# A two-layer graph network on one core: a diagonal put behind two sums, a product order, and two steps moved by one

## The chip, the cores and the metric

The kernel runs on one core of a Trainium2 chip. The metric is the device time of one execution in microseconds (us); the times shown are medians of runs. The engines of the core are TensorE (PE in the profile, its weight loads PEld), VectorE (DVE), ScalarE (ACT), GpSimd (POOL) and SyncE (SP, whose queue issues nearly all DMAs). [...]

## The reference

Sixteen graphs of 1024 nodes with 512 features share one weighted adjacency matrix. Everything is float32.

```python
# x (16, 1024, 512), adj (1024, 1024), symmetric pattern with a diagonal
h = relu(layernorm(x))                         # without scale and shift
x = x + (adj @ h) @ weight + bias              # layer 0

h  = relu(layernorm(x))                        # layer 1
g  = h @ W
s1 = g @ a[:512]; s2 = g @ a[512:]
e  = leaky_relu(s1[:, :, None] + s2[:, None, :], 0.2) * adj
x  = x + elu(softmax(e, axis=2) @ g + beta * g)
```

## The kernel before, in words

All big products are done by a scheme with seven block products in place of eight (p1 to p7, in the order p1, p2, p6, p5, p7, p3, p4 in `PRODUCTS`): a matrix is cut into 2 x 2 blocks, sums of blocks (S1 to S4 of the left side, T1 to T4 of the right) are multiplied, and the results C11, C12, C21, C22 are sums of the products. Some products use the scheme once more inside (`inner_steps`, seven small products r1 to r7).

**Layer 0** goes over the 16 batches. For each, `layer0_a2` (`layer0_a` for the first) forms adjacency times h, by pairs of products whose inner steps alternate (`products_a2`), and `layer0_b` multiplies the result by the weight (`Weighted.rest`). Tiles of this stage are called `y_...` (`y_p1y` is the PSUM tile of p1's inner products, `y_p1t` what is kept of it) and `po_...`.

**Layer 1** then goes over the 16 batches again, in `layer1`. It uses softmax(e) @ h @ W. The exponentials stay unnormalised and transposed in blocks B11, B12, B21, B22 (`pT`). `beta` times a row's sum is added onto the diagonal of these blocks (`Softmax.diagonal`), so that one product gives both terms, and rows are divided by their sums (`rs`) in the last step. `products_a` multiplies this by the normalised features (`ul_U`, `ul_S`), in tiles `z_...`; the weighted products `pq_...` follow.

The last of these, p4, is made by the seven inner steps. `with_weighted` (line 259) runs them, and one or two matmul steps of the first weighted product after each:

```python
for m in range(7):
    inn[m]()
    reads(m)
    if m > 4:
        read.last(6 - m)
    next(steps)()
    ...
    after(m)
```

For p4 the inner order is r1, r2, r5, r4, r6, r3, r7. At m = 5 (r3) VectorE forms the second block of C21 (`z_C<-z_Y,z_p4t`) and `read.last(1)` takes S4's second block from it (`z_S<-z_C,z_S`). At m = 6 (r7) ScalarE copies r7's PSUM tile, VectorE adds to it (`z_p4t<-z_p4t,in`), forms C21's first block and S4's.

The weighted products go on in `Weighted.rest`: eight matmul calls each, four for each half q of the rows, in an order of their own. It is `P5_EARLY` (p1, p5, p2, p6, p7, p3, p4) for batches 0 to 14 and `NODES_LAST` for batch 15. p5 multiplies S1 into new PSUM banks of the kind X, p2 multiplies C21 into the banks W, which p1's result has been copied to. When a half is done, `done` (line 977) acts: for p6 and p5 ScalarE copies the bank (`part`); for p7 and p3 VectorE adds the bank to such a copy (`rest`); and `elu` follows for the four output quarters.

**Order of the work around it.** While batch b is multiplied, the softmax of batch b + 1 is made on ScalarE and VectorE. Which of its steps is issued where is written out by hand: dictionaries give for a step number k a list of names, and `after(k)` issues them, after the matmuls and reads of that step. In `SOFTMAX_A` and `SOFTMAX_B` (lines 1202 to 1207) M is masking and maximum, E an exponential of 128 rows, V its transposition, X and x the exchange of maxima by DMA, N and n their use, S and s the exchange of sums, D and d the diagonals of the first and second half, T1a to T4b the right sums. Step numbers of `plan_a` count 2 for a product, so the inner steps m = 0 to 6 of p4 are 12 to 18; those of `plan_b` begin at 2 with the first product after p1. D is these instructions on VectorE (lines 857 to 869): a reduction of the exchanged sums (`sall`), a reciprocal, a product with beta, and four additions onto diagonal blocks.

Line 1309 moves the entries 0 and 1 of `plan_b` to steps 17 and 18 of `plan_a`: before the change these are D at 17 and T1a at 18.

The softmax of layer 1's first batch is prepared during layer 0 (`EARLY_B`), kept in DRAM, and finished in layer 0's last batch by `FIRST_A` and `FIRST_B`, whose steps stand among the inner steps of `products_a2` (seven for each pair of products, counted from 0). R0 to R7 reload a kept tile by a DMA on SP's queue (`er<-ed`), E and V are as above; `exp` is four activations on ScalarE, V two transpositions on VectorE.

Instructions of VectorE, ScalarE, TensorE, GpSimd and SP are kept in the program's order (class `InOrder`), and all are recorded under its line, 119. So rows of the profile are told apart by the tiles, not by lines.

Of the kernel before, what the change touches and what calls it, by code (L numbers as in the profile page):

```python
# [55 lines left out]

FORKED = tuple((*p[:4], p[4] and p[0] != "p2", p[5]) for p in PRODUCTS)

NODES_LAST = tuple(FORKED[k] for k in (0, 1, 2, 3, 5, 4, 6))

P5_EARLY = tuple(FORKED[k] for k in (0, 3, 1, 2, 4, 5, 6))

# [4 lines left out]
def kernel(  # L67
# [12 lines left out]
    B, N, D = x.shape  # L80
# [255 lines left out]
    class Weighted:  # L336
# [17 lines left out]
        def steps(self, n, left):  # L354

            prod, _, bn, kind, first, last = self.products[n]
            first = first and (kind, 0) not in self.banks

            def step(q, i, dc):
                if first and i == 0 and dc == 0:  # L360
                    self.banks[kind, q] = bank(f"{self.name}_{kind}{q}")
                ps = self.banks[kind, q].rearrange("p (i o) -> p i o", i=2)
                pe.matmul(
                    ps[:, i, :], left[:, dc, ts(2 * q + i, P)], self.w[:, W_BLOCK[bn], dc, :],
                    start=(first and i == 0 and dc == 0), stop=(last and dc == 1),
                    skip_group_check=True,
                )
                if i and dc:
                    self.done(prod, q, ps)

            return [partial(step, q, i, dc) for q in range(2) for i in range(2) for dc in range(2)]
# [538 lines left out]
    def layer1(b, plan_a, plan):  # L910
# [52 lines left out]

        products = NODES_LAST if end else P5_EARLY
        at = {p[0]: 2 * n for n, p in enumerate(products)}
# [153 lines left out]
    def merged(*plans):  # L1119
        out = {}  # L1120
        for plan in plans:
            for k, steps in plan.items():
                out.setdefault(k, []).extend(steps)
        return out
# [26 lines left out]
    def plan_out(o, b):  # L1151

        return steps(
            (-1, o.keep, 0, 1), (-1, o.keep, 1, 0), (-1, o.keep, 1, 1), (0, o.relu, 0, 0),
            (1, o.stats, 1, 0, 0), (3, o.relu, 0, 1), (4, o.stats, 1, 0, 1), (7, o.relu, 1, 0),
            (8, o.stats, 1, 1, 0), (10, o.stats, 1, 1, 1), (13, o.relu, 1, 1),
            (2, o.logits, 0, 0, 0), (3, o.logits, 0, 0, 1), (7, o.logits, 0, 1, 0),
            (8, o.logits, 0, 1, 1), (9, o.logits, 1, 0, 0), (10, inner_left, b, "p7"),
            (12, o.logits, 1, 0, 1), (13, inner_left, b, "p3"), (15, o.logits, 1, 1, 0),
            (16, o.logits, 1, 1, 1), (16, o.store_logits), (18, inner_left, b, "p4"),  # L1160
            (3, o.store, 0, 0), (6, o.store, 0, 1), (10, o.store, 1, 0), (15, o.store, 1, 1),
            (18, begin, b, "Y"), (24, begin, b, "X"),
            (8, load_res, b, 0, 0), (10, load_res, b, 0, 1), (14, load_res, b, 1, 0),
            (18, load_res, b, 1, 1),
        )
# [16 lines left out]
    def plan_softmax(order, s):  # L1182
        names = {
            "L": [s.logits], "B": [s.blocks, 0], "b": [s.blocks, 1],
            "X": [s.spread_max, 0], "x": [s.spread_max, 1], "N": [s.top, 0], "n": [s.top, 1],
            "S": [s.spread_sum, 0], "s": [s.spread_sum, 1],
            "D": [s.diagonal, 0], "d": [s.diagonal, 1],
        }
        for g in range(NCH):
            names[f"M{g}"] = [s.masked, g]  # L1190
            names[f"E{g}"] = [s.exp, g]
            names[f"V{g}"] = [s.turn, g]
            names[f"L{g}"] = [s.load, g]
            names[f"e{g}"] = [s.load, g, b4, "b4"]
            names[f"K{g}"] = [s.keep, g]
            names[f"R{g}"] = [s.reload, g]
        for n in ("T1", "T2", "T3", "T4"):
            for k in range(2):
                names[n + "ab"[k]] = [s.right_sum, n, k]
        return {k: [tuple(names[n]) for n in steps.split()] for k, steps in order.items()}  # L1200
# [3 lines left out]
        6: "N B E0", 7: "E1 V0", 8: "E2 V1", 9: "n b E3 V2 S", 10: "E4 V3", 11: "E5 E6 V4",  # L1204
        12: "E7 V5", 13: "V6 s", 15: "V7",
    }
    SOFTMAX_B = {0: "D", 1: "T1a", 2: "T1b", 4: "d", 5: "T2a", 6: "T2b"}
    LOGITS_B = {8: "L", 9: "L0", 10: "L1", 11: "e2", 12: "e3"}
    LATE_A = {5: "T3a T4a", 6: "T3b T4b"}

# [7 lines left out]
        13: {9: "N n"},  # L1218
    }
    FIRST_A = {  # L1220
        -1: "R0", 4: "E0", 8: "B V0 R1", 10: "E1", 12: "V1 R2", 17: "E2", 18: "V2 R3", 23: "E3",
        25: "b", 26: "V3 R4 R5",
    }
    FIRST_B = {
# [8 lines left out]
    for b in range(B):  # L1233
        plans = [plan_out(out_of, b)] if b else []
# [23 lines left out]
        if b == 0:  # L1258
            plan_b = merged(
                {  # L1260
                    0: [(logit_weights_back, 0), (logit_weights_back, 1)],
                    1: [(inner_right, "p7", 1)], 2: [(inner_right, "p3", 1)],
                    3: [(inner_right, "p4", 1)],
                },
                *plans_b,
            )
            layer0_a(b, merged(plan_first(), at_end(merged(*plans))))
        else:
            plan_b = merged(*plans_b)
# [10 lines left out]
    for b in range(B):  # L1280
        plans = [{
            k - 14: [(f,) for f in later.pop(k)] for k in sorted(later)
        }]
        plans.append(plan_softmax(LATE_A, sms[b]))
        plans.append(steps((7, p4_right, b, 0), (8, p4_right, b, 1), (8, p4_left, b)))
        plans.append(steps((3, u_sums, b, 0, 1), (4, u_sums, b, 1, 1)))
        plan_b = {}
        if b == 0:
            plans += [
                {6: [(w_sums, w1_c)]}, steps((-1, u_sums, b, 0, 0), (0, u_sums, b, 1, 0)),  # L1290
            ]
        if b + 1 < B:
            plans.append(plan_softmax(SOFTMAX_A, sms[b + 1]))
            plans.append({k: [(load_u, b + 1, n)] for k, n in LOADS_U.items()})
            plan_b = plan_softmax(SOFTMAX_B, sms[b + 1])
        else:
            plans.append({7 + i: [(load_x1, b, nh, q)] for i, (nh, q) in enumerate(halves)})
        if b + 2 < B:
            plan_b = merged(plan_b, plan_softmax(LOGITS_B, sms[b + 2]))
        if 1 <= b <= NCH:  # L1300
            plan_b = merged(plan_b, {
                4: [(late.load, b - 1)], 9: [(late.stats,)], 10: [(late.relu,)],
                11: [(late.logits, b - 1)], 13: [(late.store,)],
            })
            if b == NCH:
                plan_b[13].append((late.store_logits,))
        if b + 1 < B:
            plan_b = merged(plan_b, steps((10, u_sums, b + 1, 0, 0), (12, u_sums, b + 1, 1, 0)))
        plans.append({k: plan_b.pop(i) for k, i in ((17, 0), (18, 1)) if i in plan_b})
        layer1(b, merged(*plans), plan_b)  # L1310
    for k in sorted(later):
        for f in later[k]:
# [34 lines left out]
```

## Time and profile before

| | |
|---|---|
| median of 3 runs | 2280.45 us (2279.64 to 2281.96) |
| profiled execution | 2280.27 us |
| its span | 2278.4 us |
| TensorE clock granted | 0.999 |
| TensorE, busy | 2240.0 us (98%) |
| weight loads, busy | 1647.0 us (72%) |
| VectorE, busy | 1950.5 us (86%) |
| ScalarE, busy | 1547.7 us (68%) |
| GpSimd, busy | 242.9 us (11%) |
| DMA, moved | 336.07 MB |

A row of the profile names engine, operation, the tile written and the tiles read, their sizes, and how often. In lists of waits the columns are: who waited, for whom, us in total, times, the longest. In a timeline they are start and duration in us, engine, line, operation, tiles, sizes, count, and in brackets the idle time of the engine ahead of it and who ended it. Matmuls are pipelined and their ends are modelled. The span runs from the first to the last instruction; the execution's own time has 1.87 us more around it.

### The profile page before, as it was taken

The numbers are of one execution on the slowest core, as the hardware profiler recorded it, in microseconds if no ns is written. First come the engines' busy times: TensorE is split into PE (matmuls) and PEld (weight loads), VectorE is DVE, ScalarE is ACT, GpSimd is POOL, SyncE is SP. The second block draws the span as 40 slices with busy tenths as digits, with TensorE's granted clock in tenths as the row PEclk, the third lists the DMA queues.
The fourth block names the chain that finished last, engine by engine and source line by source line (L and its number), as shares of the span: only waits on it lengthen the run. The fifth ranks groups of instructions, "written<-read, shape, count | busy, mean of one in ns | idle before, by whom it ended". The sixth has DMA issues, their size and how long they took to land.

```text
span 2278.4 us, 30436 instructions
## 1 busy us (share of the span) xinstructions
PE 2240.0 (98%) x8716; PEld 1647.0 (72%) x8716; DVE 1950.5 (86%) x4477; ACT 1547.7 (68%) x4138; POOL 242.9 (11%) x508
## 2 busy tenths in 40 slices
PE   9999999999999999999999999999999999999998
PEld 5888888888888888888566556665566556665565
DVE  7888888989888898889988988889888888888864
ACT  3776776677676767676576676767766676766743
POOL 1111111111111111110000000000000000000000
PEclk9999999999999999999999999999999999999999
DMA  6343454343354444235444655556655655546541
GB/s 216 131 137 120 143 170 151 128 150 118 123 167 158 140 139 145 99 119 204 171 133 140 197 154 161 152 160 168 173 152 145 179 150 143 147 129 171 150 122 45
DMA packets 194296, 336.07 MB, mean 148 GB/s; under 512 B 78800, under 2 KB 86992, under 8 KB 194128
## 3 DMA queue, kind: packets, MB, share of 16 engines
q1 hardware_dynamic: 185168, 302.15, 40.9%
q0 software_dynamic: 8640, 31.46, 7.5%
q8 instruction: 68, 1.11, 0.2%
q14 instruction: 100, 0.82, 0.1%
q10 hardware_dynamic: 320, 0.52, 0.1%
HBM read 228.33 MB, written 109.91 MB: 148 GB/s over the span
## 4 chain that ended last, share of the span: by engine, by line
PE 77%; DVE 14%; ACT 4%; DMA 3%; issue 1%; SPq 1%; POOL 0%; DVEq 0%; ACTq 0%; POOLq 0%
PE z_Y L119 10%; PE po_Y L119 9%; PE y_Y L119 8%; PE pq_Y L119 7%; DVE pT L119 5%; PE z_X L119 5%; PE y_X L119 5%; PE po_X L119 4%; PE z_W L119 4%; PE pq_X L119 4%; PE pq_W L119 2%; PE y_W L119 2%; PE y_p7y L119 2%; PE y_p3y L119 2%; DVE z_C L119 2%; PE y_p6y L119 2%
## 5 line engine op out<-in xcount | busy, mean ns | idle before, releaser
L119 ACT ACTIVATE e<-e,nm 128x256 f32<-128x256 f32 x480 | 236.8, 498 | 51.4 <-DVE nm L119 51.4
L119 DVE CUSTOM_DVE_ANT_0 e<-e,mask 128x256 f32<-128x256 f32 x512 | 200.0, 424 | 54.0 <-ACT e L119 46.9
L119 PE MATMUL z_Y<-pT,ul_U 128*128 128x512 f32 x512 | 225.0, 592 | 0.0
L119 ACT ACTIVATE e<-s2b,s1b 128x256 f32<-128x256 f32 x512 | 214.7, 499 | 0.0
L119 PE MATMUL pq_Y<-w_c,z_C 128*128 128x256 f32 x768 | 189.1, 379 | 0.0
L119 PE MATMUL po_Y<-w_c,y_C 128*128 128x256 f32 x768 | 188.3, 379 | 0.0
L119 PEld LDWEIGHTS z_Y<-pT,ul_U 128*128 128x128 f32 x512 | 97.4, 190 | 115.5 <-issue 111.4
L119 DVE CUSTOM_DVE_ANT_0 y_S<-xr,v_bc 128x512 f32<-128x512 f32 x240 | 165.4, 689 | 9.2 <-DVE s L119 0.5
L119 PEld LDWEIGHTS po_Y<-w_c,y_C 128*128 128x128 f32 x768 | 146.1, 190 | 20.1 <-issue 0.5
L119 PEld LDWEIGHTS pq_Y<-w_c,z_C 128*128 128x128 f32 x768 | 146.1, 190 | 19.7
L119 DVE STREAM_TRANSPOSE pT<-e 128x512 f32<-128x512 f32 x240 | 150.8, 681 | 1.4
L119 PE MATMUL pq_X<-w_c,z_S 128*128 128x256 f32 x512 | 119.8, 383 | 19.5 <-DVE z_C L119 19.5
L119 ACT ACTIVATE h<-h,nb_h,r_h 128x512 f32<-128x512 f32 (+1 forms) x132 | 98.2, 792 | 57.3 <-POOL nb_h L119 57.3
L119 PEld LDWEIGHTS pq_X<-w_c,z_S 128*128 128x128 f32 x512 | 95.9, 190 | 38.6 <-DVE z_C L119 26.3
L119 ACT ACTIVATE y_S<-xr 128x512 f32<-128x512 f32 x90 | 56.7, 630 | 92.9 <-DVE xr L119 92.5
L119 POOL DMA_DIRECT2D o<-x1d x60 | 52.7, 935 | 620.3 <-DVE o L119 557.6
L119 PE MATMUL po_X<-w_c,y_S 128*128 128x256 f32 x512 | 115.7, 379 | 0.0
L119 PE MATMUL z_X<-pT,ul_S 128*128 128x512 f32 x256 | 112.5, 592 | 0.0
L119 PE MATMUL z_W<-pT,ul_U 128*128 128x512 f32 x256 | 112.5, 592 | 0.0
L119 PE MATMUL z_Y<-pT_T,ul_S 128*128 128x512 f32 x256 | 112.5, 592 | 0.0
L119 PE MATMUL z_X<-pT_T,ul_S 128*128 128x512 f32 x256 | 112.5, 592 | 0.0
L119 PEld LDWEIGHTS po_X<-w_c,y_S 128*128 128x128 f32 x512 | 97.4, 190 | 13.1
(259 smaller groups left out, 5240.2 us busy)
## 6 DMA issues: line engine op xcount, KB each, us to landing
mask<-maskd SPq DMA_DIRECT2D x128, 512.0 KB
h<-in_x_dram SPq DMA_DIRECT2D x64, 512.0 KB
xr<-in_x_dram SPq DMA_DIRECT2D x256, 128.0 KB
x1d<-xr SPq DMA_DIRECT2D x64, 512.0 KB
ul_U<-ud_U SPq DMA_DIRECT2D x64, 512.0 KB
ud_U<-xr SPq DMA_DIRECT2D x60, 512.0 KB
o<-x1d POOLq DMA_DIRECT2D x60, 512.0 KB, 8.1
out_dram<-o SPq DMA_DIRECT2D x240, 128.0 KB
```

What stands on the lines that cost most here:

```text
L119: return lambda *args, **kwargs: tc.keep_in_program_order(f(*args, **kwargs))
```

## The change

Three edits to the written-out order; no instruction is added or removed.

1. `SOFTMAX_B` puts D at 1, T1a at 2 and T1b at 3 in place of 0, 1 and 2, and line 1309 moves the entry 1 alone, to step 18. So D is issued at the end of step 18, behind the sums of r7, where it was at 17, ahead of them. T1a is issued at step 2 instead of 18, T1b at 3 instead of 2.
2. `NODES_LAST`, the order of the weighted products of the last batch, becomes p1, p5, p2, p6, p3, p7, p4; it was p1, p2, p6, p5, p3, p7, p4.
3. `FIRST_A` has E0 at step 5 instead of 4, and V2 with the reload R3 at 19 instead of 18.

```diff
-NODES_LAST = tuple(FORKED[k] for k in (0, 1, 2, 3, 5, 4, 6))
+NODES_LAST = tuple(FORKED[k] for k in (0, 3, 1, 2, 5, 4, 6))
...
-    SOFTMAX_B = {0: "D", 1: "T1a", 2: "T1b", 4: "d", 5: "T2a", 6: "T2b"}
+    SOFTMAX_B = {1: "D", 2: "T1a", 3: "T1b", 4: "d", 5: "T2a", 6: "T2b"}
...
     FIRST_A = {
-        -1: "R0", 4: "E0", 8: "B V0 R1", 10: "E1", 12: "V1 R2", 17: "E2", 18: "V2 R3", 23: "E3",
+        -1: "R0", 5: "E0", 8: "B V0 R1", 10: "E1", 12: "V1 R2", 17: "E2", 19: "V2 R3", 23: "E3",
         25: "b", 26: "V3 R4 R5",
     }
...
-        plans.append({k: plan_b.pop(i) for k, i in ((17, 0), (18, 1)) if i in plan_b})
+        plans.append({18: plan_b.pop(1, [])})
         layer1(b, merged(*plans), plan_b)
```

## The prediction

> **What bounds the kernel now.** I read the first and second part of the page, then what TensorE waited for, then the stretch around the longest of these waits.
>
> ```profile
> PE 2240.0 (98%) x8716; PEld 1647.0 (72%) x8716; DVE 1950.5 (86%) x4477; ACT 1547.7 (68%) x4138; POOL 242.9 (11%) x508
> PEclk9999999999999999999999999999999999999999
> ```
>
> TensorE is occupied throughout at full clock. So time can be won only where it stands still. All its waits, with releasers:
>
> ```profile
> PE pq_X L119 <- DVE z_C L119: 19.5, 15, 1.4
> ...
> PE pq_W L119 <- DVE z_C L119: 1.2, 1, 1.2
> PE z_p4y L119 <- ACT z_p4t L119: 1.2, 1, 1.2
> PE y_p3y L119 <- DVE y_p3t L119: 1.2, 1, 1.2
> ...
> PE y_p6y L119 <- ACT y_p1t L119: 0.8, 1, 0.8
> ```
>
> The first row is layer 1: one stop in each of batches 0 to 14, each 1.28 to 1.39 us. The second is the same place in batch 15. The last two are in layer 0's last batch, at 1067.81 and 1042.50. The third is layer 1's first batch, at 1144.15. The timeline of VectorE, then of TensorE, at one of the fifteen:
>
> ```profile
> 1661.77 0.69 DVE L119 TENSOR_TENSOR z_C<-z_Y,z_p4t 128x512 f32<-128x512 f32 x1
> 1662.49 0.69 DVE L119 TENSOR_TENSOR z_S<-z_C,z_S 128x512 f32<-128x512 f32 x1
> 1663.10 0.17 DVE L119 TENSOR_REDUCE sz<-sall 128x4 f32<-128x16 f32 x1
> 1663.31 0.18 DVE L119 RECIPROCAL rs<-sz 128x4 f32<-128x4 f32 x1
> 1663.41 0.20 DVE L119 TENSOR_SCALAR sz<-sz,beta_c 128x4 f32<-128x4 f32 x1
> 1663.64 1.14 DVE L119 SCALAR_TENSOR_TENSOR pT<-ident,sz,pT 128x128 f32<-128x128 f32 x4
> 1664.70 0.42 DVE L119 TENSOR_TENSOR z_p4t<-z_p4t,in 128x256 f32<-128x256 f32 x1
> 1665.15 0.69 DVE L119 TENSOR_TENSOR z_C<-z_Y,z_p4t 128x512 f32<-128x512 f32 x1
> ```
>
> ```profile
> 1662.72 1.89 PE L119 MATMUL pq_X<-w_c,z_S 128*128 128x256 f32 x8
> 1665.90 0.70 PE L119 MATMUL pq_X<-w_c,z_S 128*128 128x256 f32 x2 [1.28 <-DVE z_C L119]
> ```
>
> The two `z_C<-z_Y,z_p4t` are C21's two blocks. Between them stand seven short instructions, the diagonal of the next batch's first half ("D"). p5's first half (`pq_X`) runs on after the first block; its second half waits until 1665.90, for the second block at 1665.84.
>
> [...] what stands ahead in VectorE's program delays C21, as this trace shows (1.60 us from 1663.10 to 1664.70). [...] p5 doesn't read C21, so the wait is for the bank that C21's add reads, and the trace agrees (releaser `z_C<-z_Y,z_p4t`). [...]
>
> **Layer 1, batches 0 to 14.** D moves behind both C21 blocks and their S4 sums; T1's halves move from steps 18 and 2 to 2 and 3. VectorE does the same instructions in another order; no DMA moves.
> What a stop costs is more than its idle time. Matmuls of 256 columns follow each other every 0.216 us, but one's modelled duration is 0.379, so 0.163 us of a stop are not counted as idle; and the first matmul after a wait is followed after 0.320 instead of 0.216 us, 0.104 more. A stop costs idle + 0.267 us. Check: a batch has 96 matmuls of 512 columns (1536 in 16 batches, 6.87 us for 16) and 140 of 256: 41.2 + 30.2 = 71.4 us. The stops lie 72.96 apart (1884.80, 1957.76): 1.55 lost, and 1.28 + 0.267 = 1.55.
> What takes its place: S4 starts at 1662.49, the next VectorE slot is 0.61 later (1663.10), `z_p4t` then (its input, ScalarE's copy of 0.37 us from 1662.49, is there at 1662.87), the C21 block 0.45 later, 1663.55 to 1664.24, TensorE free to load weights at 1664.28 and effectively to multiply 0.10 later, at 1664.39. Its first half ends its issue at 1662.72 + 8 x 0.216 = 1664.45. So the stop vanishes, with 0.06 us to spare; where the first half began late too (0.32 instead of 0.216 at its start) it stays within 0.1. Sum: 19.5 + 15 x 0.267 = 23.5, less some 0.2 for the narrow ones: **23.3 us**. Bounds: 19.5 less 15 x 0.1 = 18 below, 23.5 above.
> What hides D now: VectorE from 1663.9 to the first wait in the weighted products. It does S4, D, T1a, T1b, d in one stretch to about the same absolute time as before; then it waits for p7:
>
> ```profile
> DVE z L119 <- PE pq_Y L119: 3.8, 2, 2.7
> DVE e L119 <- ACT e L119: 2.9, 4, 1.1
> DVE o L119 <- ACT z L119: 1.1, 1, 1.1
> DVE z_C L119 <- PE z_X L119: 0.6, 1, 0.6
> ```
>
> These are all VectorE's waits from 1593 to 1666. The longest, 2.7 us, shrinks by 1.55 to 1.2 as TensorE comes earlier; after it everything keeps its place to TensorE. The row sums for D have landed (D starts 0.61 after S4, without a wait), and d's too (it starts at 1668.76 behind T1 without one). T1 is wanted by p5 of the next batch, more than 20 us on. ScalarE's wait for p5's second half (2.7 to 2.8 us) shrinks likewise. If this cover were gone, each us of VectorE beyond 1.2 would cost a us per batch.
>
> **The last batch of layer 1** has no D; p2 reads C21 itself, which comes at 2247.78, and TensorE stops 1.21 us. p5 reads S1, ready since 2239; its first half needs the bank of C21's first block (read by 2245.62) and can start at 2246.46, its second at 2248.18, after 2247.83. p2 follows at 2249.9. Gain 1.21 + 0.267 = **1.5**. What is behind moves along: p2's eight activations (0.36 us apart, 2.9 us) come one product (3.45 us) later, but p3's first sum comes after VectorE's 5.9 us of idleness, so the end keeps its distance to TensorE.
>
> **Layer 0's last batch.** E0 (ScalarE, 1040.12 to 1042.10, waiting 0.62 for its reload) stands ahead of the eviction of p1's tile, for which TensorE stops 0.80. One step later it stands behind that and C11's copy, but ahead of p2's eviction: 1040.8 to 1042.8, eviction to 1043.13, p5's first matmul due at 1043.26: just in time. So TensorE gains 0.80 + 0.267 = 1.07 there. But VectorE, idle 2.84 before 1042.48, then works without a break over 0.14 us to 1064.08, and at 1058.6 TensorE waits for a copy of its result. Its work starts again with p2's second sum, behind the eviction just costed: 1043.17 instead of 1043.68. So only **0.5** arrives.
> V2 (two transposes, 1.21 us) stands ahead of the `y_p3t` sum; behind p7's sums it frees TensorE at 1066.6 instead of 1067.81, 1.2. Yet VectorE's work stays the same, and into layer 1's first batch it is never idle but for 1.0 and 1.6 us (a mask's landing) until 1165; TensorE waits there anyway (1.20 at 1144.15, ScalarE behind exponentials that wait 5.7 for VectorE's maximum). So I count V2 at **0**. R3, on SP's queue, waits for V2's buffer: 1.96 later (three sums and an add of 0.3 to 0.6 us pass ahead), and layer 1's four loads behind it too. It landed at 1071.14 for an exponential at 1072.70: 0.4 late at worst, where ScalarE later idles 2.3. Bounds for the whole: 0.5 lost to 0.80 + 1.18 + 2 x 0.267 = 2.5 won.
>
> **Sum.** 23.3 + 1.5 + 0.5 = 25.3 us. The profiled execution has a span of 2278.4 and took 2280.27, 1.87 around it; the median of the runs is 2280.45, 0.2 above. 2278.4 - 25.3 + 1.9 = **2255.0 us**.
>
> **Rivals.**
> (a) As forecast, 0.77; 2253.3 to 2257.
> (b) A smaller wait takes the place of the stop: p5's second half misses by 0.5 us per batch, as the margin is 0.06, or VectorE's 1.2 us of slack is partly used. 15 x 0.5 = 7.5 back: 2262.5. For it: the narrow margin; against: each term above is a row of this trace. 0.09.
> (c) Layer 0's two stops arrive in full: 2.0 more, 2253.0. For: VectorE's 1.0 and 1.6 us of idleness could take some; against: the mask's landing is a DMA's time. 0.08.
> (d) D waits, once it is late, with T1, d and the `o` sums behind it, so that p7's sums become the bound. VectorE's slack there is 1.2 after the gain; slower than before by 0.2% (4.6 us) needs 25.3 + 4.6 = 29.9 over 15 batches, 2.0 per batch, so a delay above 3.2 us. Priced at 3.5: 2284.5. Against: the sums are there before D's old place. 0.03.
> (e) The stop has another cause that comes at the same time (p5's bank freed by something else): only 2 us are won, 2278.5. Against: fifteen times the same releaser, 0.04 us before. 0.03.
>
> **Range and chances.** What this kernel's measurement can tell from no change is about 0.2%, 4.6 us. (a), (c) hold 0.85 and, with (c)'s lower edge and a residual of 0.1 to 0.2 us per stop, give 2252.5 to 2259. Faster are (a), (b), (c): 0.94; same (e): 0.03; slower (d): 0.03.
>
> **What would show it.** TensorE's row `pq_X <- DVE z_C` gone or below 0.2 us each, the stops of `pq_X` 71.4 us apart where 72.96 were; VectorE's order C21, S4, `z_p4t`, C21, S4, `sz`; its wait for `pq_Y` near 1.2. `pq_W <- z_C` gone at the end. `y_p6y` and `y_p3y` gone, but `z_p4y` longer than 1.2. It would be wrong if a new row of TensorE's waits comes fifteen times, or if VectorE waits for `sall`.

## The result, and the profile after

The changed kernel takes 2254.87 us (2254.63 to 2254.97, 4 runs) against 2280.65 us (2279.64 to 2281.96, 4 runs) of the kernel before on the same chip: a ratio of 0.9886, 95% interval 0.9869 to 0.9904. The forecast was 2255.0, the range 2252.5 to 2259.0. The profiled execution took 2254.63 with a span of 2252.7; before it was 2280.27 and 2278.4.

The first part of the page of the kernel after (busy time, share of the span, count):

```profile
PE 2236.1 (99%) x8716; PEld 1645.5 (73%) x8716; DVE 1950.3 (87%) x4477; ACT 1547.9 (69%) x4138; POOL 243.7 (11%) x508
```

The counts are those of before, and VectorE and ScalarE have the same work (1950.5 and 1547.7 before). The span became 25.6 us shorter, TensorE's busy time only 3.9: it did the same matmuls and stood less. All that TensorE waited for longer than 0.15 us after the change (who, for whom, us in total, times, longest):

```profile
PE y_Y L119 <- ACT adjT_B L119: 1.8, 1, 1.8
PE warm L119 <- POOL ident masks.py:199: 1.4, 1, 1.4
PE z_p4y L119 <- ACT z_p4t L119: 1.2, 1, 1.2
PE adjt L119 <- ACT adjT_B L119: 0.9, 1, 0.9
PE y_p4y L119 <- DVE y_p4t L119: 0.5, 1, 0.5
PE y_p5y L119 <- DVE y_p5t L119: 0.2, 1, 0.2
```

The row `pq_X <- DVE z_C`, 19.5 us in fifteen stops, is gone without a successor that repeats. `pq_W <- z_C`, `y_p3y` and `y_p6y` are gone too, `z_p4y` is as it was, and two short ones are new: `y_p4y` and `y_p5y`, both in layer 0's last batch. The other three rows belong to the start, before the stages that were changed.

The timeline of VectorE in the batch that the prediction showed, now 12 us earlier (start, duration, operation), then the line of TensorE's p5 in it:

```profile
1649.57 0.69 DVE L119 TENSOR_TENSOR z_C<-z_Y,z_p4t 128x512 f32<-128x512 f32 x1
1650.30 0.69 DVE L119 TENSOR_TENSOR z_S<-z_C,z_S 128x512 f32<-128x512 f32 x1
1650.91 0.42 DVE L119 TENSOR_TENSOR z_p4t<-z_p4t,in 128x256 f32<-128x256 f32 x1
1651.36 0.69 DVE L119 TENSOR_TENSOR z_C<-z_Y,z_p4t 128x512 f32<-128x512 f32 x1
1652.09 0.69 DVE L119 TENSOR_TENSOR z_S<-z_C,z_S 128x512 f32<-128x512 f32 x1
1652.70 0.17 DVE L119 TENSOR_REDUCE sz<-sall 128x4 f32<-128x16 f32 x1
```

```profile
1650.53 3.62 PE L119 MATMUL pq_X<-w_c,z_S 128*128 128x256 f32 x16
```

The second `z_C<-z_Y,z_p4t` now starts 1.79 after the first (1651.36 - 1649.57), where it was 3.38, and D begins behind both (`sz<-sall`), 0.61 after S4's second block and without idle time in brackets, so it doesn't wait for its sums. p5's sixteen matmuls run through: the second half's start is no longer a row of its own with idle time in brackets.

What took the place of the cover: VectorE's waits from 1634 to 1706, which take in one whole period.

```profile
DVE e L119 <- ACT e L119: 2.9, 4, 1.1
DVE z L119 <- PE pq_Y L119: 2.2, 2, 1.2
DVE o L119 <- ACT z L119: 1.1, 1, 1.1
DVE z_C L119 <- PE z_X L119: 0.6, 1, 0.6
```

Three rows are as before, and the one for p7's `pq_Y` went from 3.8 (longest 2.7) to 2.2 (longest 1.2): VectorE gave up idle time that it had, and by as much as the stop was long.

The last batch, TensorE's timeline: p5 and then p2 follow p1 without a gap, where p2 had stopped 1.21.

```profile
2221.86 3.62 PE L119 MATMUL pq_X<-w_c,z_S 128*128 128x256 f32 x16
2225.32 3.62 PE L119 MATMUL pq_W<-w_c,z_C 128*128 128x256 f32 x16
```

Starts of the same instructions in the two profiles cut the 25.6 us into stages:

| stage of TensorE's work | before | after | difference |
|---|---|---|---|
| start to layer 0's last batch (its first `y_p1y`) | 1029.45 | 1029.21 | -0.24 |
| to its first `po_X` | 48.83 | 48.13 | -0.70 |
| to layer 1's first `pq_X` | 73.04 | 73.08 | +0.04 |
| to the last batch's p4 (`z_p4y`), fifteen stops | 1085.65 | 1061.96 | -23.69 |
| to the end of TensorE's work | 31.86 | 30.38 | -1.48 |
| to the end of the span | 9.57 | 10.00 | +0.44 |

The first and the last rows have no edit in them. The last lies between 9.55 and 10.0 in the profiles of this study, the start varies too; both are taken as scatter.

### The profile page after: what moved, and what is told of

The parts are those of the page before. It is cut to its first block, busy times and chain, and to the rows that moved or that the text cites. A ratio compares the mean times of both kernels' runs of the same rounds, so it can differ in the third digit from the quotient of the medians.

```text
span 2252.7 us, 30436 instructions
## 1 busy us (share of the span) xinstructions
PE 2236.1 (99%) x8716; PEld 1645.5 (73%) x8716; DVE 1950.3 (87%) x4477; ACT 1547.9 (69%) x4138; POOL 243.7 (11%) x508
## 4 chain that ended last, share of the span: by engine, by line
PE 96%; DVE 2%; ACT 1%; DMA 1%; issue 0%; POOL 0%; SPq 0%; DVEq 0%; POOLq 0%
PE z_Y L119 16%; PE po_Y L119 10%; PE pq_Y L119 9%; PE z_X L119 9%; PE y_Y L119 8%; PE po_X L119 5%; PE z_W L119 5%; PE pq_X L119 5%; PE y_X L119 4%; PE y_W L119 3%; PE y_p7y L119 2%; PE pq_W L119 2%; PE po_W L119 2%; PE z_p4y L119 2%; PE y_p3y L119 2%; PE y_p4y L119 2%
```

## The experiments

All are made from one of the two kernels, and each was timed beside the kernel before on its chip: 2280.37 (31 runs) in the first group, 2280.61 (7) in the second, 2280.84 (7) in the third.

### The parts alone

**D behind C21 alone**, the diff's edits of `SOFTMAX_B` and of the entries moved to step 18, in the kernel before:

```diff
-    SOFTMAX_B = {0: "D", 1: "T1a", 2: "T1b", 4: "d", 5: "T2a", 6: "T2b"}
+    SOFTMAX_B = {1: "D", 2: "T1a", 3: "T1b", 4: "d", 5: "T2a", 6: "T2b"}
...
-        plans.append({k: plan_b.pop(i) for k, i in ((17, 0), (18, 1)) if i in plan_b})
+        plans.append({18: plan_b.pop(1, [])})
```

> The kernel before with the diagonal's edit alone (SOFTMAX_B and the line that moves its entries to steps 17 and 18). Theory (VectorE's order holds back the bank that p5's second half needs): TensorE's fifteen stops at pq_X vanish, 23.3 us less, about 2257.3 us; the stop at pq_W of the last batch (1.2) and the two in layer 0 stay. Rival (the stop has another cause, and the 25.8 us come from layer 0's edits shifting everything): within 3 us of before. Rival (a smaller wait takes its place when the other edits are missing): 2262 us or more.

2258.78 us (2256.18 to 2261.57, 4 runs), a ratio of 0.9905 (0.9891 to 0.992). The median is 1.5 us above the 2257.3 of the theory; the four runs lie 5.4 us apart, and the profile is that of the fastest. From the first `pq_X` to the last batch's p4 the profile has 23.35 us less than before. Three of TensorE's waits in it:

```profile
PE pq_W L119 <- DVE z_C L119: 1.2, 1, 1.2
PE z_p4y L119 <- ACT z_p4t L119: 1.2, 1, 1.2
PE y_p3y L119 <- DVE y_p3t L119: 1.2, 1, 1.2
```

So the stop of p5 goes with this edit alone, and the stops of the last batch and of V2 are others: they stand as they were.

**The last batch's order alone**:

```diff
-NODES_LAST = tuple(FORKED[k] for k in (0, 1, 2, 3, 5, 4, 6))
+NODES_LAST = tuple(FORKED[k] for k in (0, 3, 1, 2, 5, 4, 6))
```

> The kernel before with the last batch's product order alone. Theory: the one stop at pq_W (1.21 us idle, 1.48 with the restart) vanishes and the tail moves along: 1.5 us less, 2279.1 us, and the distance from TensorE's last matmul to the end of the span stays as before. Rival (ScalarE's eight activations of p2, one product later, crowd p3's and push the end): the stop vanishes, the span stays within 0.5 us of before.

2278.70 us (2277.87 to 2282.49, 12 runs), a ratio of 0.9995 (0.9986 to 1.0003). By the times alone this can't be told from nothing, as 1.5 us are 0.07%. The profile tells it: from the last p4 to the end of TensorE's work 30.38 us, 1.48 less than before, and as long as in the changed kernel. The profiled execution was the longest of the twelve, for a reason far from the edit: a tile of the mask landed 1.6 us later than in the profile before, and `z_p4y`'s stop was 3.29 instead of 1.20.

**E0 one step later, alone**:

```diff
-        -1: "R0", 4: "E0", 8: "B V0 R1", 10: "E1", 12: "V1 R2", 17: "E2", 18: "V2 R3", 23: "E3",
+        -1: "R0", 5: "E0", 8: "B V0 R1", 10: "E1", 12: "V1 R2", 17: "E2", 18: "V2 R3", 23: "E3",
```

> The kernel before with the first exponential of layer 0's last batch at step 5, the transpose left at 18. Theory: TensorE's stop at y_p6y (0.80) vanishes, but VectorE's chain behind it comes only 0.5 us earlier, so layer 1's first weighted matmul comes 0.5 us earlier (apart from what differs before 1030 us): 2280.1 us. Rival (the stop's whole 0.80 + 0.27 arrives): 1.1 us less. Rival (p2's eviction, now behind the exponential, stops TensorE instead): no gain, a new row for y_p5y.

2280.49 us (2279.45 to 2284.37, 12 runs), a ratio of 1.0003 (0.9994 to 1.0012). No stop at `y_p6y`, a new one of 0.21 at `y_p5y`. From the last batch's first `y_p1y` to its first `po_X` it took 48.25 us, 0.58 less than in the profile of before, as the theory had it. But with the last batch's order alone, where E0 is at its old place, it took 48.10. Why is shown below, with V2's profile.

**V2 and R3 one step later, alone**:

```diff
-        -1: "R0", 4: "E0", 8: "B V0 R1", 10: "E1", 12: "V1 R2", 17: "E2", 18: "V2 R3", 23: "E3",
+        -1: "R0", 4: "E0", 8: "B V0 R1", 10: "E1", 12: "V1 R2", 17: "E2", 19: "V2 R3", 23: "E3",
```

> The kernel before with the transpose V2 and its reload R3 at step 19, the first exponential left at 4. Theory: the stop at y_p3y (1.18) falls to about 0.1, TensorE runs 1.2 us earlier until VectorE, whose work is unchanged, holds it again within some 10 us (new rows at y_p4y or y_Y, together about 1 us); layer 1 begins at most 0.2 us earlier. Rival (the gain lasts until the stop at z_p4y, which grows from 1.2 to 2.4): no new row before 1143. Rival (it arrives in full): 1.2 to 1.4 us less.

2279.78 us (2279.12 to 2280.82, 12 runs), a ratio of 0.9995 (0.9987 to 1.0004). The `y_p3y` stop is gone: TensorE begins the next small product 37.40 us after the batch's first `y_p1y`, where it was 38.60 with the last batch's order alone: 1.20 earlier. (That profile is the fair one to compare with; the profile of before had lost more time ahead of this point, as is shown below.) Nine microseconds on, TensorE's timeline has

```profile
1075.97 1.13 PE L119 MATMUL y_p4y<-adjT_T,h 128*128 128x256 f32 x4 [0.45 <-DVE y_p4t L119]
```

and another stop of 0.08 at 1070.94. With 0.267 for each restart that is 0.53 + 0.53 = 1.06 of the 1.20 given back, to VectorE, which still has V2's two transpositions to do, now behind the sums and no longer ahead of them. 0.14 is left at `po_X` (47.96 against 48.10).

This profile also explains E0. ScalarE's first activation of E0 in the kernel before, and in this one, where E0 is at its old place as well:

```profile
1040.12 0.51 ACT L119 ACTIVATE er<-er,nm 128x256 f32<-128x256 f32 x1 [0.62 <-DMA er<-ed]
```

```profile
1039.36 0.49 ACT L119 ACTIVATE er<-er,nm 128x256 f32<-128x256 f32 x1
```

In the first E0 waits for its reload R0; in the second R0 is there and E0 doesn't wait. The stop at `y_p6y` behind it was 0.80 in the first and 0.07 in the second. In the profiles with E0 at step 4 the reload landed between 1038.67 and 1038.90 four times (stop 0.07) and at 1040.09 and 1040.16 twice (0.80 and 0.93). So this stop isn't in every execution. In the two profiles of the changed kernel R0 landed late as well (1039.89 and 1040.44), but E0, one step later, didn't wait for it.

### The whole again, and what can be taken from it

**The changed kernel again** (no edit), and **without both of layer 0's edits** (the `FIRST_A` of before), on one chip:

> The changed kernel once more, to see how its executions scatter: before scatters from 2279.1 to 2282.6 us, and the profiles differ in when one mask lands in layer 1's first batch. Theory (the scatter is that landing, which the change doesn't touch): a scatter of 2 to 3 us above 2254.6. Rival (the edits in layer 0 keep the landing off the path): all within 0.5 us of 2254.8.

> The changed kernel without the two edits in layer 0. Theory (they bring some 0.3 to 0.7 us and no more): 2255.2 to 2255.6 us in the fastest executions. Rival (they are worth 2.4 us, which is what the diagonal's edit alone, 2258.8, less 1.5 for the last batch, leaves to 2254.9): 2257.3.

The first: 2255.08 us (2254.91 to 2255.32, 4 runs), 0.9887 (0.9872 to 0.9902). The second: 2257.11 us (2254.77, 2256.80, 2257.42, 2257.45), 0.9897 (0.988 to 0.9913). Its fastest execution is as fast as the changed kernel's, the other three are 2 us longer. That execution is the one with a profile, where R0 was early; in what the three others were longer isn't seen. Of the expectations, the rival held for the changed kernel, whose executions lie within 0.4 us here. Without layer 0's edits the median fits the rival and the fastest execution the theory.

**Without V2's edit alone, and without E0's alone**, each in the changed kernel:

```diff
-        -1: "R0", 5: "E0", 8: "B V0 R1", 10: "E1", 12: "V1 R2", 17: "E2", 19: "V2 R3", 23: "E3",
+        -1: "R0", 5: "E0", 8: "B V0 R1", 10: "E1", 12: "V1 R2", 17: "E2", 18: "V2 R3", 23: "E3",
```

```diff
-        -1: "R0", 5: "E0", 8: "B V0 R1", 10: "E1", 12: "V1 R2", 17: "E2", 19: "V2 R3", 23: "E3",
+        -1: "R0", 4: "E0", 8: "B V0 R1", 10: "E1", 12: "V1 R2", 17: "E2", 19: "V2 R3", 23: "E3",
```

> The changed kernel without V2's move (E0 stays moved). Without both moves the executions lay at 2254.8, 2256.8, 2257.4 and 2257.5 us, with both eight of eight between 2254.6 and 2255.3. Theory one (V2's move, with R3 and four loads behind it on SP's queue, makes the difference in when the masks land in layer 1's first batch): as without both, a median near 2257. Theory two (E0's move, which takes a reload's landing off TensorE's path, makes it): median near 2255.

> The changed kernel without E0's move (V2 stays moved). Theory one (V2's move makes the executions regular): median near 2255, scatter below 1 us. Theory two (E0's move makes it): as without both, a median near 2257, and the stop at y_p6y in the profile.

Without V2's edit 2255.01 us (2254.83, 2254.94, 2255.08, 2257.57), 0.9891 (0.9876 to 0.9905); without E0's 2255.22 us (2254.52, 2254.89, 2255.55, 2256.14), 0.9888 (0.9872 to 0.9905). In the profile without E0's edit R0 was late, and TensorE waited

```profile
PE y_p6y L119 <- ACT y_p1t L119: 0.9, 1, 0.9
```

Against the changed kernel's second profile this costs 0.70 us at `po_X` (48.83 us from the batch's first `y_p1y`, against 48.13). It follows from the parts: the stop of 0.93 + 0.267 stands against a stop of 0.22 + 0.267 at `y_p5y` that the changed kernel has in its place, 1.20 - 0.49 = 0.71.

Both medians are near 2255: either move alone gives the median of both, so neither theory singles one out. With both edits twelve of twelve executions (the changed kernel twice, and the last experiment below) lie within 0.7 us of each other for their kernel; in the three kernels that have one of them or none beside the other edits they spread over 1.6 to 2.7 us. Whether the edits make it so, and which, is not settled: four executions each are few, one of each has a profile, and one further kernel with both edits (T1a's, below) had an execution that began 2 us later than the others.

### What D's new place costs and what covers it

**Something short in D's old place.** Two small VectorE instructions that change nothing (a product of `ident` with 1, 0.40 us for both) at step 17 of the changed kernel, in batches 0 to 14:

```diff
+    def busy():
+        for _ in range(2):
+            dve.tensor_scalar(ident, ident, 1.0, None, op0=ALU.mult)
...
+        if b + 1 < B:
+            plans.append({17: [(busy,)]})
```

> The changed kernel with two short multiplications by one (ident by 1.0 into itself) on VectorE at step 17, where the diagonal stood, in batches 0 to 14. Theory (the place in VectorE's order is what counts, and the margin is 0.06 us): if the two take x us, TensorE stops again at pq_X in all fifteen, each costing x - 0.06 with the restart; for x = 0.5 that is 6.6 us. Rival (it was the diagonal's own data or its wait for the sums): no stop, no time. Rival (the margin is 0.3 or more): under 3 us.

2260.77 us (1 run), span 2258.9. VectorE's timeline at the place:

```profile
1654.65 0.48 DVE L119 TENSOR_SCALAR ident<-ident 128x128 f32<-128x128 f32 x2
1655.04 0.42 DVE L119 TENSOR_TENSOR z_p4t<-z_p4t,in 128x256 f32<-128x256 f32 x1
```

`z_p4t` starts at 1655.04, 0.4 us behind the slot at 1654.65 that it had without the filler. TensorE's p5 in this batch takes 3.97 us, where it takes 3.62 in the changed kernel:

```profile
1654.27 3.97 PE L119 MATMUL pq_X<-w_c,z_S 128*128 128x256 f32 x16
```

From the first `pq_X` to the last p4 it took 1067.75 us, 5.80 more than the changed kernel, 0.39 per batch. In thirteen of the fifteen batches p5's second half starts 0.46 to 0.48 after the matmul ahead of it instead of 0.216, and the next one 0.320 after that: some 0.35 lost of the 0.40 put ahead of C21. So 0.05 us are free, near the 0.06 of the prediction. In the two others p5's first half comes late too, and the loss is larger. VectorE took the filler where the program has it: `z_p4t` started 1.00 us after the S4 sum ahead of it (1655.04 - 1654.04), 0.61 in the changed kernel (1650.91 - 1650.30), and TensorE lost 0.39 per batch. The run also prices a restart: the thirteen stops have 0.08 to 0.10 us of idle time each (all fifteen 1.48, most of them too short for the lists of waits), and 0.08 + 0.267 = 0.35.

**T1a back in the step of D**, with T1b at 2, in the changed kernel:

```diff
-    SOFTMAX_B = {1: "D", 2: "T1a", 3: "T1b", 4: "d", 5: "T2a", 6: "T2b"}
+    SOFTMAX_B = {1: "D T1a", 2: "T1b", 4: "d", 5: "T2a", 6: "T2b"}
```

> The changed kernel with the halves of T1 at their old steps 18 (behind the diagonal) and 2. Theory: VectorE's order around C21 is the same, no new stop, within 0.5 us of the changed kernel. Rival (T1's later place is part of the gain): a stop of up to 1.1 us per batch, 16 us.

2257.27 us (1 run), of which 2.0 to 2.4 us lie at the start of that execution: the first `y_p1y` of layer 0's last batch starts at 1031.64, where the other profiles have 1029.2 to 1029.7. The stage that has the edit took 1061.91 us, the changed kernel's 1061.96. So T1's place costs nothing and wins nothing; D's place alone counts. (The times of this and of the two fillers are of one execution each; the comparison by stages doesn't hang on where that execution began.)

**VectorE's slack.** Ten of the same instructions, 2.53 us, at step 4 ahead of d, in batches 0 to 14:

```diff
+    def busy():
+        for _ in range(10):
+            dve.tensor_scalar(ident, ident, 1.0, None, op0=ALU.mult)
...
+        if b + 1 < B:
+            plan_b = merged({4: [(busy,)]}, plan_b)
```

> The changed kernel with ten multiplications of ident by one on VectorE at step 4 of the weighted products, ahead of the second half's diagonal, in batches 0 to 14; by the runs with two, some 0.25 us each, 2.5 us in all, of which VectorE's wait for p7 (1.17 us) covers the first part. Theory as the prediction put it (each us of VectorE beyond 1.2 costs a us per batch): 1.3 x 15 = 20 us more, 2275 us. Rival (what is late is p7's sum, whose bank TensorE needs only in the next batch, and VectorE has 2.1 us more of waits behind it, so that the delay is gone before TensorE asks): within 1 us of the changed kernel.

2265.80 us (1 run), span 2263.9. The stage took 1073.20 us, 11.2 more than after the change, 0.75 per batch. Neither theory has that. A new row among TensorE's waits, and in ScalarE's timeline and VectorE's what lies behind it:

```profile
PE pq_Y L119 <- ACT z L119: 7.0, 15, 0.5
```

```profile
1668.05 0.59 ACT L119 COPY z<-pq_Y 128x512 f32<-128x512 f32 x1 [2.65 <-DVE o L119]
```

```profile
1667.28 0.68 DVE L119 SCALAR_TENSOR_TENSOR o<-ez,o 128x512 f32<-128x512 f32 x1
```

It isn't the wait for p7's sums that decides. By the releasers, ScalarE waits 2.65 us for VectorE's `o<-ez,o`, which gives a buffer back, before it copies p6's second half out of its bank (`z<-pq_Y`, 1668.05); p7's second half is to be written to that bank, and TensorE waits for the copy (0.46 in this batch, until 1668.69). The stop is 7.0 / 15 = 0.47, with its restart 0.74, near the 0.75 measured. So 2.53 us cost 0.75, and the slack is 1.8 us, not 1.2, by another chain than the one that had been read.

### A version that is faster than both

**The weight's sums of layer 1's first batch later.** With the changed kernel only one larger stop is left in the region, `z_p4y` (1.24). ScalarE's copy for it stands behind exponentials that wait for VectorE's maximum, and VectorE has four subtractions (`w_sums`, 2.61 us for `w_c<-w_c`) just ahead of that maximum. They are needed later only. The first goes to step 12, the three others to step 18:

```diff
-    def w_sums(w):
+    def w_sums(w, parts=(0, 1)):
...
-        add(t1, b12, b11, ALU.subtract)
-        add(t2, b22, t1, ALU.subtract)
-        add(b12, b22, b12, ALU.subtract)
-        add(t4, b21, t2, ALU.subtract)
+        if 0 in parts:
+            add(t1, b12, b11, ALU.subtract)
+        if 1 in parts:
+            add(t2, b22, t1, ALU.subtract)
+            add(b12, b22, b12, ALU.subtract)
+            add(t4, b21, t2, ALU.subtract)
...
-                {6: [(w_sums, w1_c)]}, steps((-1, u_sums, b, 0, 0), (0, u_sums, b, 1, 0)),
+                {12: [(w_sums, w1_c, (0,))], 18: [(w_sums, w1_c, (1,))]}, steps((-1, u_sums, b, 0, 0), (0, u_sums, b, 1, 0)),
```

> The changed kernel with layer 1's weight sums (four subtractions, 2.4 us on VectorE, done once, at step 6 of the first batch ahead of the maxima) moved: the first to step 12, the other three to step 18 ahead of the diagonal. Theory (TensorE's last large stop, z_p4y, 1.2 to 1.7 us, is ScalarE's exponentials, late since they wait for VectorE's maxima): the maxima come 2.4 us earlier, the stop goes, 1.2 + 0.27 = 1.5 us less, 2253.4 us. Rival (the masks' landing and VectorE's backlog hold that batch anyway): the stop moves to C21's first block or stays, less than 0.4 us gained.

2253.53 us (2253.38 to 2253.67, 4 runs), a ratio to the kernel before of 0.9882 (0.9867 to 0.9896), span 2251.7. ScalarE's first exponential behind the maximum, in the changed kernel and in this one:

```profile
1128.58 0.51 ACT L119 ACTIVATE e<-e,nm 128x256 f32<-128x256 f32 x1 [5.71 <-DVE nm L119]
```

```profile
1126.45 0.51 ACT L119 ACTIVATE e<-e,nm 128x256 f32<-128x256 f32 x1 [3.13 <-DVE nm L119]
```

The wait is 2.58 shorter. `z_p4y`'s stop is gone, a stop of 0.23 at `pq_X` is new, and from the first `po_X` of layer 0's last batch to the first `pq_X` it took 71.81 us instead of 73.08: 1.27 less. The stop was worth 1.24 + 0.267 = 1.51. The one at `pq_X` is only in part new: in the changed kernel that matmul already came 0.372 after the one ahead of it, where 0.216 is the rule, too little to count as idle time; now it comes after 0.613. 1.51 - (0.613 - 0.372) = 1.27. All four executions are below all eight of the changed kernel.

## Why the prediction was right, and where it was not

**Layer 1, 23.3 us: 23.7 measured.** Fifteen times 1.58. The term held by mechanism and by size: D's edit alone gave 23.35, T1's place nothing, and a filler in D's old place brought a loss back, 0.35 of its 0.40 in thirteen batches of fifteen. "A stop costs idle + 0.267 us" is needed for it: 19.5 of idle time were worth 23.7, and the stops of 0.08 to 0.10 and of 0.47 that the fillers made fit too. The 0.2 that the prediction took off for narrow ones did not appear in the profile of the changed kernel. VectorE's wait for p7 was forecast at 1.2 and is 1.2. That p5 waited for a bank is read from the releaser and from the pool that both tiles come from; the runs show that C21's add ended the wait, and no address. Too few buffers were not the cause: the same buffers serve without the stops, fifteen and 19.5 us before, when seven instructions stand elsewhere.

**The last batch, 1.5 us: 1.48 measured**, and the same with that edit alone. TensorE's end moved by it, and the tail after it kept its length within its scatter.

**Layer 0, 0.5 us: 0.70 measured** in the profiles, with several of its sentences wrong or right for one execution alone. So the nearness is in part luck: where R0 is early with layer 0 as it was (D's edit or the last batch's order alone), the stage to `po_X` takes 48.10, and 48.13 after the change is no gain.
- "E0 (...) stands ahead of the eviction of p1's tile, for which TensorE stops 0.80": so in the profile of before, because R0 landed late in it. In four other profiles the reload was 1.2 to 1.4 us earlier and the stop 0.07. The edit wins 0.6 to 0.7 where R0 is late (48.83 to 48.25 alone, to 48.13 beside V2's) and costs 0.15 where it is early (48.25 against 48.10). That VectorE swallows part of TensorE's gain was right; it shows as the stop of 0.22 at `y_p5y`, at 1052.89, not at 1058.6.
- V2's gain, "So I count V2 at 0": near to right as a number (0.14), wrong as to place. The prediction let it be lost at layer 1's first batch, with "`z_p4y` longer than 1.2". `z_p4y` was 1.24 against 1.20, since nothing came that far: VectorE's own sums for `y_p4y` took it back within 10 us, in the stop at 1075.9, which the prediction had not listed.
- "R3, on SP's queue, waits for V2's buffer: 1.96 later" was wrong: R3 was issued at 1066.14 after the change and at 1067.51 before, 1.37 earlier, and ahead of V2, which starts at 1067.32. So it didn't wait for V2's buffer there, and the price for its being late fell away.
- That `z_p4y` waits for VectorE's maximum by way of ScalarE was right, and the last experiment won 1.3 us from it.

**The cover, "each us of VectorE beyond 1.2 would cost a us per batch"**, failed. 2.53 us cost 0.75: the slack is 1.8, and the chain that ends it runs over a buffer, ScalarE's copy and p6's bank. The prediction read VectorE's longest wait, which tells when VectorE is idle, not who is late next. This step priced rival (d) and decided nothing, as D didn't wait. The price of (d) is also wrong by its own rule: a delay of 3.5 us would cost (3.5 - 1.2) x 15 = 34.5 us and give 2289.5, not 2284.5.

The rivals: of (b) there is no trace in the changed kernel; the filler in D's old place shows what 0.40 us would have done, so the margin was real. (c), layer 0's stops in full, priced 2.5 us for layer 0; 0.70 came by the stages, though the medians with and without layer 0's edits lie 2.0 apart, which isn't explained. (e) fell with D alone.

**The sum, 25.3 us: 25.6 measured in the span**, 23.69 + 1.48 + 0.70 = 25.9 by stages, with -0.24 and +0.44 of scatter at start and end. The single edits' medians add up to less: (2280.37 - 2258.78) + (2280.37 - 2278.70) + (2280.37 - 2279.78) + (2280.37 - 2280.49) = 21.59 + 1.67 + 0.59 - 0.12 = 23.7, with 25.8 for the whole. The 2 us between are about what the median of the kernel without layer 0's edits is longer (2257.11 against 2255.08). What makes three of its executions longer, and whether either edit prevents it, stays open. With such a scatter, the 0.1 us between the forecast and the median is luck; what holds is the sum by stages.

## What to carry to other kernels

When an engine's program has other work between two halves of a result that the bounding engine waits for, count how much idle time that engine has later in the period, and put the other work there: seven short instructions at another step were worth 1.58 us per batch. Price a repeated stop from the distance between its repetitions, not from its idle time alone (1.28 idle, 1.55 lost here), and take a stop seen in one profiled execution for a constant only where nothing in it hangs on a DMA's landing (the one at `y_p6y` was 0.80 in one profile and 0.07 in another). For slack, follow what is released by the delayed engine to the next waiter, and test it with a filler of known length; the engine's own longest wait can name the wrong chain (it read 1.2 here, where the filler gave 1.8).

## What the runs showed of the hardware that was not expected

- A stop of TensorE, among these matmuls of 256 columns, costs 0.27 us beyond its idle time, also where the idle time is only 0.08: thirteen stops of the filler in D's old place cost 0.35 each, and one of 0.08 in the changed kernel (`y_Y`, 1070.90) 0.34: its first matmul started 0.455 after the one ahead of it and the next 0.320 after that, where such matmuls start 0.216 apart in the median of that profile.
- The landing of a 512 KB load differs from execution to execution of nearly the same program while other loads run. R0 landed between 1038.67 and 1040.16 in six profiles whose batch began within 0.1 us of each other. The mask tile of layer 1's preparation was used at 1113.6 in one profile of the changed kernel and at 1116.6 in that of the last batch's order alone, after a wait of 3.91 us for its DMA, and TensorE's stop at `z_p4y` then was 3.29 instead of 1.2.
